# An attention loop in longer runs: two product runs and two runs of ten score tiles a slot

## The chip, the cores and the metric

The kernel runs on one core of one Trainium2 chip. The core has five engines that run side by side, each through its own queue in order: TensorE (PE in the profile, with its weight loads as PEld), VectorE (DVE), ScalarE (ACT), GpSimd (POOL) and SyncE (SP), which here only issues DMAs. The metric is the device time of the whole kernel in microseconds (us), the median of several runs.

## The reference

A transformer block on x of 8 batches, 1024 tokens and 512 features, all in fp32. First attention, then a mixture of eight experts:

```python
x = x + attention(layernorm(x))
x = x + experts(layernorm(x))

# attention: 16 heads of 32 features
theta_q = xh / (1 + abs(w_q)) + b_q + t * phi_q      # likewise theta_k; theta_v has no t
Q = concat(cos(theta_q), sin(theta_q))               # 64 features a head; K likewise
V = cos(theta_v) + sin(theta_v)
attn = softmax(causal(Q @ K.T / sqrt(64)))
theta_out = (attn @ V) / (1 + abs(w_out)) + b_out
return cos(theta_out) + sin(theta_out)

# experts: softmax router, the best two of eight, at most 160 tokens an expert and batch
h = relu(buf @ W1[e] + b1[e]); y = h @ W2[e] + b2[e]   # weighted and summed per token
```

Sine and cosine come from a table of 2048 entries with linear interpolation. The kernel computes them as an angle, a square and a hardware sine.

## The kernel before

**Work and stages.** The attention part is a loop of 32 **slots** (line 1736), n = 4b + c: batch b, and c one of four groups of 128 features, that is four heads. Two heads make a **pair**; a slot has pair 0 and pair 1. After the loop comes the expert part (`experts`), which the change leaves alone. For batch b - 1 a **router** runs inside the slots of batch b, as a generator that is advanced a step at a time (`route_on`, line 1764).

**Order.** VectorE, ScalarE, TensorE and SyncE have a manual schedule: each engine runs its instructions exactly in the order in which the Python code emits them. The code is therefore an order written out by hand. Generators are used to emit pieces of one piece of work between pieces of another: `some(k, g)` emits k steps, `rest(g)` all that are left. Waits between engines follow from the tiles that the instructions read and write.

**Scores.** `scores` (line 675) makes ten tiles for a pair: three for the first half of the queries, seven for the second. A tile is a set of matmuls (line 684) of 64 rows of the array, the two heads beside each other, on the diagonal also a mask product in bf16 (line 698), into a PSUM slot of two banks (`two_banks`, pool `ps_sc` of **three slots**, used in rotation), and one exp on ScalarE (line 704) into a tile `e` in SBUF. Transposes, the router's features and the router's sums use the same three slots.

**Products.** `attend` (line 710) multiplies the `e` tiles by v (line 718), 64 columns of the array a head, sums in PSUM, and one VectorE operation brings the result out (`av_sb`, line 726). One call makes half of the queries of a pair. `turn` (line 742) transposes a pair's two results on TensorE (line 216) and divides by the sums on VectorE (lines 753 and 755).

**Places.** `qk_pre` (line 508) transposes x for a later slot (line 216), and four VectorE operations (line 525) make angles in `qk_f`. `angle` (line 438) makes `qk_r`. `both` emits on ScalarE two squares (line 442) and two absolutes (line 585), `qk_sin` the sines (lines 594 and 445). `qk_post` (line 599) multiplies cosine half and sine half on VectorE (line 448), each followed by four DMAs that bring the result into the pair tiles `qk` for the scores. The position part of the angle comes by DMA (`load_base`, line 500).

**v and the output.** `v_pre` (line 619) has three VectorE operations for the angle and one shift; `sine`, `square` on ScalarE and `v_post` (line 639) finish v. `o_pre` (line 643) and `o_post` (line 651) do the same for the attention's output, with the residual and the statistics for the second layernorm (line 661).

**The router** (line 787): statistics and rows on VectorE (lines 798, 813), `features` transposes rows (line 216) and copies them out on VectorE (line 838), `sums` multiplies by the router's weights (line 875) and gathers (line 858) with copies on VectorE (lines 880, 882), then the choice of two experts and a product for each token's place (line 858 again, read at lines 966 and 967). It begins in the slot with c = 0 (`begin`), and the next slot finds `begin` set.

The profile shows two table loads a slot on ScalarE (1283 ns each), one ahead of the sines and one ahead of the exps that follow them.

Of the kernel before, what the change touches and what calls it, by code (L numbers as in the profile page):

```python
# [12 lines left out]
F32 = mybir.dt.float32  # L13
# [9 lines left out]
P = 128  # L23
# [51 lines left out]
def preln_attn_moe_kernel(  # L75
# [21 lines left out]
    nc = tc.nc  # L97
# [612 lines left out]
    def attend(n, pr, h, es, halves):  # L710

        vt = v_tiles[n % 2]
        av = ps_av.tile([P, 512], F32, name="av")
        tiles = tiles_of(h)
        for i, parts in enumerate(tiles):
            for kb, q0, w, at in parts:
                for a in range(2):
                    nc.tensor.matmul(  # L718
                        av[a * 64 : (a + 1) * 64, q0 - 512 * h :],
                        lhsT=vt[:, kb, 2 * pr + a, :], rhs=es[i][:, a, at : at + w],  # L720
                        start=kb == 0, stop=i + 1 == len(tiles),
                    )
# [1008 lines left out]
    last = None  # L1731
    o_st = route = first_rows = None
    begin = False
    place, angles, residual = [None], iter(()), iter(())
    first_gather = gather(0)
    for n in range(NCK):
        more, late = n + 1 < NCK, last is not None
        b, c = divmod(n, NCH)
        if n == NCK - 1:
            to_inputs.close()  # L1740
            first_rows = experts_begin()
        pos_n = trig.tile([P, S], F32, name="o_p")
        if n == NCK - 2:
            find_rows(0)
            next(first_gather)
        if late:
            e11, halves1, pos = last
# [33 lines left out]
        if n == 0:  # L1781
            some(2, *ahead)
        if n == 0 or begin:

            qk_st = rest(qk_pre(n + 1))
            if begin:
                v_post(n, v_st)
                next(route)
            angle(*qk_st)
            angles = keep(place, both(qk_st))  # L1790
            if begin:
                load_base(n + 2)

        if begin:
# [7 lines left out]
        if begin:  # L1802
            rest(asides.pop(0))
            v_st = v_box[0]
        elif more:
            v_st = v_box[0]
# [6 lines left out]
        if begin:  # L1813
# [11 lines left out]
        route_on(1)  # L1825
        if n == 2:
            load_b1()
        if c == 3 and b > 0:
            next(route)
            if b > 1:  # L1830
                fetch_slots(b - 2)
            if b < B - 1:
                scatter()


        some(3, *products)
        if n == 0:
# [23 lines left out]
        if late:  # L1861
            square(o_st[0])
            residual = o_post(n - 1, o_st)
        some(2, *ahead)
        begin = c == 0 and late
        if begin:
            rest(residual)
            route = router(b - 1)
            next(route)
        elif n + 2 < NCK:  # L1870
            route_on(1)
            qk_st = rest(qk_pre(n + 2))

        if c != 1:
            next(residual, None)
        if n + 2 < NCK and not begin and c != 1:
            angle(*qk_st)
        if c != 1:
            rest(residual)
        if c == 1:  # L1880
# [6 lines left out]
        route_on(1)  # L1887
        if c == 1:

            angle(*qk_st)  # L1890
        some(5, *ahead)
        if n + 2 < NCK and not begin:
            angles = keep(place, both(qk_st))
            some(2, angles)
            if n + 3 < NCK:
                load_base(n + 3)
        last = (es[1], halves1, pos_n)
# [62 lines left out]
```

## Time and profile before

| what | value |
|---|---|
| median of 3 runs | 3190.2 us (3189.37 to 3190.49) |
| the profiled execution | 3177.95 us, span 3176.2 us |
| granted TensorE clock | 0.998 |
| TensorE busy | 3112.0 us, 98% |
| VectorE busy | 2303.7 us, 73% |
| ScalarE busy | 1680.4 us, 53% |
| exps, line 704 | 569.4 us in 640 |
| score matmuls, line 684 | 598.3 us in 3072 |
| product matmuls, line 718 | 523.4 us in 3072 |

The profiled execution is one run and was 0.4% under the median of the others. Busy times are unions: where two matmuls run beside each other in two halves of the array they count once. A row of the profile names the line, the engine, the operation, what it writes and reads, the shape, how often it came (x), the busy time and the mean of one in ns, and the idle time before it with what ended it. A line of the timeline gives start, duration, engine, line, operation and count of merged instructions, and in brackets how long the engine was idle before and what released it. A busy TensorE can hold hidden waits, since the ends of matmuls are modelled; the starts are measured.

### The profile page before, as it was taken

How to read it: one execution, taken by the hardware profiler on the slowest of the kernel's cores; microseconds unless marked ns; L12 is line 12 of the kernel's file. 1: busy time of each engine (PE TensorE's matmuls, PEld its weight loads, DVE VectorE, ACT ScalarE, POOL GpSimd, SP SyncE). 2: the span in 40 equal slices, each digit the busy share in tenths (PEclk: the TensorE clock that was granted, in tenths of full speed). 3: DMA queues.
4: the chain of work that ended last, by engine and by line, in shares of the span. 5: the costliest groups of instructions: out<-in, count | busy, mean ns of one | idle time of the engine just before them, and what ended most of it. 6: DMA issues, size and time to landing. Idle time of an engine off the chain costs nothing.

```text
span 3176.2 us, 52225 instructions
## 1 busy us (share of the span) xinstructions
PE 3112.0 (98%) x20086; PEld 2147.5 (68%) x20086; DVE 2303.7 (73%) x4808; ACT 1680.4 (53%) x2599; POOL 424.1 (13%) x387
## 2 busy tenths in 40 slices
PE   5999999999999999999999999999999999999998
PEld 2444444444444444689699699699698698698697
DVE  8888878887887775738658658658667767767765
ACT  7888888888888885413423423423423423423423
POOL 3000202020201122410110110110110110110010
PEclk9999999999999999999999999999999999999999
DMA  5535454555545352533523523523533433433421
GB/s 167 147 100 166 106 165 132 148 138 149 164 133 160 80 167 55 149 82 96 155 54 91 152 57 95 145 59 98 140 64 100 132 67 102 128 67 108 118 58 23
DMA packets 288552, 358.79 MB, mean 113 GB/s; under 512 B 28376, under 2 KB 199088, under 8 KB 276272
## 3 DMA queue, kind: packets, MB, share of 16 engines
q1 hardware_dynamic: 264944, 312.20, 33.7%
q0 software_dynamic: 22912, 43.22, 7.3%
q8 instruction: 160, 2.62, 0.4%
q14 instruction: 88, 0.72, 0.1%
q10 hardware_dynamic: 448, 0.02, 0.0%
HBM read 207.02 MB, written 81.22 MB: 91 GB/s over the span
## 4 chain that ended last, share of the span: by engine, by line
PE 78%; DVE 4%; ACT 1%; issue 1%; DMA 0%; SPq 0%; POOLq 0%; POOL 0%; DVEq 0%; ACTq 0%
PE ps_p L1238 30%; PE ps_p L1474 10%; PE ps_p L1537 10%; PE av L718 10%; PE ps_s L684 9%; PE ps_p L1352 8%; ACT e L704 1%; PE ps_s L216 1%; PE ps_s L698 1%; DVE qk_f L525 1%; DVE qk_r L448 0%; DMA qk<-qk_r 0%; DVE xT L838 0%; DVE xe L1174 0%; DVE xe_s L1186 0%
## 5 line engine op out<-in xcount | busy, mean ns | idle before, releaser
L704 ACT ACTIVATE e<-ps_s 128x1024 f32<-128x1024 f32 (+1 forms) x640 | 569.4, 937 | 183.5 <-PE ps_s L684 110.0
L684 PE MATMUL ps_s<-qk 64*128 64x512 f32 (+3 forms) x3072 | 598.3, 506 | 28.2 <-DMA qk<-qk_r 12.4
L718 PE MATMUL av<-e,v 128*64 128x512 f32 (+3 forms) x3072 | 523.4, 490 | 0.0
L684 PEld LDWEIGHTS ps_s<-qk 64*128 64x128 f32 x3072 | 262.3, 188 | 216.0 <-issue 106.9
L718 PEld LDWEIGHTS av<-e,v 128*64 128x64 f32 x3072 | 200.5, 137 | 283.0 <-issue 267.0
L1238 PE MATMUL ps_p<-xe,w 128*128 128x256 f32 (+1 forms) x1024 | 317.6, 433 | 1.1 <-issue 1.1
L1238 PE MATMUL ps_p<-xe_s,t 128*128 128x256 f32 (+1 forms) x1024 | 317.6, 433 | 0.0
L1238 PE MATMUL ps_p<-xe,t 128*128 128x256 f32 (+1 forms) x1024 | 317.6, 433 | 0.0
L1316 POOL DMA_INDIRECT out_dram<-y,slots x80 | 127.8, 1597 | 1261.3 <-ACT y L1311 1017.8
L769 POOL DMA_INDIRECT slot_d<-token,slot x128 | 156.6, 1223 | 997.3 <-issue 620.8
L1238 PEld LDWEIGHTS ps_p<-xe_s,t 128*128 128x128 f32 x1024 | 194.4, 190 | 81.4 <-issue 0.8
L1238 PEld LDWEIGHTS ps_p<-xe,t 128*128 128x128 f32 x1024 | 194.2, 190 | 80.4 <-issue 0.4
L1238 PEld LDWEIGHTS ps_p<-xe,w 128*128 128x128 f32 x1024 | 193.7, 190 | 79.4 <-issue 1.2
L1281 DVE TENSOR_TENSOR hid<-hid 128x256 f32<-128x256 f32 (+1 forms) x128 | 63.9, 499 | 206.4 <-ACT hid L1279 206.4
L1537 PE MATMUL ps_p<-w_t,hid 128*128 128x256 f32 x960 | 212.4, 379 | 0.8 <-DVE y L1590 0.8
L1537 PEld LDWEIGHTS ps_p<-w_t,hid 128*128 128x128 f32 x960 | 180.0, 190 | 24.4 <-DVE y L1590 1.2
L1238 PE MATMUL ps_p<-xe_s,w 128*128 128x256 f32 (+1 forms) x512 | 158.9, 433 | 0.6 <-ACT p L1254 0.6
L1352 PE MATMUL ps_p<-w,hid 128*128 128x256 f32 x640 | 142.9, 379 | 0.0
L1474 PE MATMUL ps_p<-w,hid 128*128 128x128 f32 x1104 | 141.8, 275 | 0.0
L698 PEld LDWEIGHTS <-keys_b 64*128 64x128 bf16 x1536 | 80.9, 95 | 89.7 <-issue 71.8
L1311 ACT ACTIVATE y<-y,slots 128x256 f32<-128x256 f32 (+1 forms) x120 | 65.9, 578 | 142.8 <-DVE y L1389 105.5
L1474 PEld LDWEIGHTS ps_p<-w,hid 128*128 128x128 f32 x1104 | 135.8, 192 | 2.3
(289 smaller groups left out, 5182.7 us busy)
## 6 DMA issues: line engine op xcount, KB each, us to landing
w<-in_L_ffn_W_dram SPq DMA_DIRECT2D x256, 256.0 KB, 3.4
w<-in_L_ffn_W_dram SPq DMA_DIRECT2D x64, 512.0 KB, 6.8
qk<-qk_c SPq DMA_DIRECT2D x124, 256.0 KB, 4.5
qk<-qk_r SPq DMA_DIRECT2D x120, 256.0 KB, 4.9
qk_base<-base_d SPq DMA_DIRECT2D x28, 1024.0 KB, 8.8
xn_d<-xn SPq DMA_DIRECT2D x72, 256.0 KB, 2.3
rows_d<-xg SPq DMA_DIRECT2D x70, 256.0 KB, 2.1
x_mid<-in_L_attn_x_dram SPq DMA_DIRECT2D x16, 1024.0 KB, 9.2
```

The source lines that it names most:

```text
L684: nc.tensor.matmul(ps[:, a, at : at + w], lhsT=pair[r, 1, kb * P : (kb + 1) * P], rhs=pair[r, 0, q0 : q0 + w], start=at == 0, stop=not own ...
L698: nc.tensor.matmul(out_, lhsT=keys_b[r, part, :], rhs=late, start=False, stop=part == 1, skip_group_check=True,)
L704: nc.scalar.activation(e, ps[:, :, :n], AF.Exp, scale=UNIT * UNIT / math.sqrt(2 * DH))
L718: nc.tensor.matmul(av[a * 64 : (a + 1) * 64, q0 - 512 * h :], lhsT=vt[:, kb, 2 * pr + a, :], rhs=es[i][:, a, at : at + w], start=kb == 0, ...
L769: queued = nc.gpsimd.indirect_dma_start(out=slot_d[b], out_offset=bass.IndirectOffsetOnAxis(ap=idx, axis=0), in_=src, in_offset=None,)
L1238: nc.tensor.matmul(ps, lhsT=weights[:, k, :], rhs=rows[:, k, :], start=first and k == 0, stop=last and k == 1, skip_group_check=True,)
L1281: TT(g1, g3, h22, ALU.add)
L1311: nc.scalar.activation(part, part, AF.Identity, scale=meta[:, e, jj[r], 1:2].bitcast(F32))
L1316: ins = nc.gpsimd.indirect_dma_start(out=out, out_offset=bass.IndirectOffsetOnAxis(ap=meta[:, e, jj[r], 0:1], axis=0), in_=y, in_offset=No ...
L1352: nc.tensor.matmul(ps, lhsT=hid[:, k, part, cols], rhs=ws[weight][:, k, :], start=first and k == 0, stop=last and k == NHQ - 1, skip_group ...
L1474: nc.tensor.matmul(ps, lhsT=left[:, k, :], rhs=right[:, k, :], start=first and k == 0, stop=k == 3, skip_group_check=True,)
L1537: nc.tensor.matmul(ps[:, b * DC : (b + 1) * DC], lhsT=hid[:, k, part, b * P : (b + 1) * P], rhs=ws[weight][:, k, :], start=first and k == ...
```

## The change

The loop is put in another order. No instruction of the computation is added or taken away, except one: an exp of one element, emitted after the sines in every slot but the first.

- **Products.** Before, four runs a slot: the first three tiles of what was left of the slot before's pair 1, later its last four; all ten of pair 0 beside the sines; the first three of pair 1 inside its scores. After, two runs: all of the slot before's pair 1 at the start of a slot, all of pair 0 in the middle.
- **Scores.** Before, runs of five tiles with products between. After, ten tiles in a row for each pair, with the VectorE work of asides, residual and router steps emitted between them.
- **Transposes.** `qk_pre` for the next slot and `turn` of the slot before's pair 0 go ahead of the first product run. Before, `qk_pre` ran a slot sooner, in the second score run, and `turn` of pair 0 stood there too.
- **Squares and places.** `square` of v, `square` of o (now of slot n - 2's output), and `both` are emitted ahead of the first product run. In the slot where the router begins, and in the last, the square of o stays in the second score run.
- **v.** `v_pre` is emitted a slot sooner, behind `v_post` in the second score run; where `begin` is set, both come at the start of the slot, behind `angle`.
- **DMAs.** `load_base` goes to the start of the slot, `load_mid` stays in the second score run. The last half of `qk_post`, with its four DMAs, is emitted straight after the middle product run, ahead of the router's step there.

```diff
         products = [attend(n, 0, h, es[h], halves[0]) for h in range(2)]
-        if late:
-            products.insert(0, attend(n - 1, 1, 1, e11, halves1))
         ahead = [scores(pairs[0], h, es[h]) for h in range(2)]
-        v_box = [None]
-        asides = [keep(v_box, v_pre(n + 1))] if more else [first_rows]
+        asides = [] if more else [first_rows]
...
+        if n == 0:
+            some(2, *ahead)
+        if more:
+            qk_st = rest(qk_pre(n + 1))
         if late:
-            some(3, *products)
-        route_on(1)
+            es1, halves1, halves0 = last
+            pos = trig.tile([P, S], F32, name="o_p")
+            turn(0, halves0, pos)
+        if more:
+            angle(*qk_st)
+        if begin:
+            v_post(n, v_st)
+            v_st = rest(v_pre(n + 1))
+        if n and n + 2 < NCK:
+            load_base(n + 2)
+        if n == 2:
+            load_mid(b)
+        if late:
+            if more and not begin:
+                square(v_st[0])
+            if n > 1 and not begin:
+                square(o_st[0])
+                residual = o_post(n - 2, o_st)
+            if more:
+                rest(keep(place, both(qk_st)))
+            for h in range(2):
+                rest(attend(n - 1, 1, h, es1[h], halves1))
+        for _ in range(2):
+            route_on(1)
+        route_on(2)
+        with_asides(1)
         route_on(2)
         if c == 2 and route is not None:
             asides.append(part(route))
...
-        if begin:
-            some(5, *ahead)
-        else:
-            with_asides(5)
+        with_asides(4)
         rest(residual)
         for _ in range(2):
             route_on(1)
-        rest(angles)
...
+        if n == 0 or begin:
             square(v_st[0])
-        if late:
-            some(4, *products)
-        route_on(1)
-        route_on(1)
-        with_asides(5)
-        if begin:
-            square(v_st[0])
+        with_asides(2)
+        for _ in range(2):
+            route_on(1)
+        with_asides(3)
...
         if late:
             sine(o_st[1])
+        if n:
+            nc.scalar.activation(warm, split_c, AF.Exp)
...
         some(NTT, *products)
-
-        es, halves1 = [[], []], []
-        ahead = [scores(pairs[1], h, es[h]) for h in range(2)]
+        next_pairs = rest(post) if more else None
+
+        es1, halves1 = [[], []], []
+        ahead = [scores(pairs[1], h, es1[h]) for h in range(2)]
         route_on(1)
         route_on(2)
-        some(2, *ahead)
-        turn(0, halves[0], pos_n)
-        next_pairs = rest(post) if more else None
-        some(1, *ahead)
-        if late:
+        some(3, *ahead)
+        begin = c == 0 and late
+        if begin or not more:
             square(o_st[0])
-            residual = o_post(n - 1, o_st)
-        some(2, *ahead)
-        begin = c == 0 and late
+            rest(o_post(n - 1, o_st))
         if begin:
-            rest(residual)
             route = router(b - 1)
             next(route)
-        elif n + 2 < NCK:
-            route_on(1)
-            qk_st = rest(qk_pre(n + 2))
...
+        some(2, *ahead)
+        route_on(1)
+        if c == 1 and b > 0:
             load_mid(b)
...
         if more and not begin:
             v_post(n + 1, v_st)
-        some(3, attend(n, 1, 0, es[0], halves1))
...
+            if n + 2 < NCK:
+                v_st = rest(v_pre(n + 2))
         some(5, *ahead)
...
+        last = (es1, halves1, halves[0])
         pairs = next_pairs
-    rest(attend(NCK - 1, 1, 1, es[1], halves1))
+    pos_n = trig.tile([P, S], F32, name="o_p")
+    turn(0, halves[0], pos_n)
+    for h in range(2):
+        rest(attend(NCK - 1, 1, h, es1[h], halves1))
     turn(1, halves1, pos_n)
```

More of the change, by code (lines that the diff above doesn't have):

```diff
@@ L1733, in preln_attn_moe_kernel @@
     begin = False
-    place, angles, residual = [None], iter(()), iter(())
+    place, residual = [None], iter(())
     first_gather = gather(0)
@@ L1741, in preln_attn_moe_kernel @@
             first_rows = experts_begin()
-        pos_n = trig.tile([P, S], F32, name="o_p")
         if n == NCK - 2:
@@ L1745, in preln_attn_moe_kernel @@
             next(first_gather)
-        if late:
-            e11, halves1, pos = last
         es, halves = [[], []], [[], []]
         products = [attend(n, 0, h, es[h], halves[0]) for h in range(2)]
-        if late:
-            products.insert(0, attend(n - 1, 1, 1, e11, halves1))
         ahead = [scores(pairs[0], h, es[h]) for h in range(2)]
-        v_box = [None]
-        asides = [keep(v_box, v_pre(n + 1))] if more else [first_rows]
+        asides = [] if more else [first_rows]
         if b == 0 and c in (1, 2):
@@ L1780, in preln_attn_moe_kernel @@
             asides.append(part(route))
-        if n == 0:
-            some(2, *ahead)
-        if n == 0 or begin:
-            qk_st = rest(qk_pre(n + 1))
-            if begin:
[L1787 to L1790, printed above, removed]
-            if begin:
-                load_base(n + 2)
-        if begin:
-            some(5, *ahead)
-        else:
-            with_asides(5)
+        with_asides(4)
         rest(residual)
@@ L1800, in preln_attn_moe_kernel @@
             route_on(1)
-        rest(angles)
[L1802 to L1806, printed above, removed]
-            square(v_st[0])
-        if late:
-            some(4, *products)
-        route_on(1)
-        route_on(1)
-        with_asides(5)
-        if begin:
-            square(v_st[0])
+        if n == 0:
+            rest(keep(place, both(qk_st)))
+            v_st = rest(v_pre(1))
+        if n == 0 or begin:
+            square(v_st[0])
+        with_asides(2)
+        for _ in range(2):
+            route_on(1)
+        with_asides(3)
         for g in asides:
@@ L1823, in preln_attn_moe_kernel @@
             o_st = o_pre(n - 1, pos)
-        route_on(1)
-        route_on(1)
+        for _ in range(2):
+            route_on(1)
         if n == 2:
@@ L1851, in preln_attn_moe_kernel @@
         some(NTT, *products)
-        es, halves1 = [[], []], []
-        ahead = [scores(pairs[1], h, es[h]) for h in range(2)]
+        next_pairs = rest(post) if more else None
+        es1, halves1 = [[], []], []
+        ahead = [scores(pairs[1], h, es1[h]) for h in range(2)]
         route_on(1)
         route_on(2)
-        some(2, *ahead)
-        turn(0, halves[0], pos_n)
-        next_pairs = rest(post) if more else None
-        some(1, *ahead)
-        if late:
+        some(3, *ahead)
+        begin = c == 0 and late
+        if begin or not more:
             square(o_st[0])
-            residual = o_post(n - 1, o_st)
-        some(2, *ahead)
-        begin = c == 0 and late
+            rest(o_post(n - 1, o_st))
         if begin:
-            rest(residual)
             route = router(b - 1)
             next(route)
-        elif n + 2 < NCK:
-            route_on(1)
-            qk_st = rest(qk_pre(n + 2))
[L1874 to L1880, printed above, removed]
+        some(2, *ahead)
+        route_on(1)
+        if c == 1 and b > 0:
             load_mid(b)
@@ L1885, in preln_attn_moe_kernel @@
             v_post(n + 1, v_st)
-        some(3, attend(n, 1, 0, es[0], halves1))
-        route_on(1)
-        if c == 1:
-            angle(*qk_st)
+            if n + 2 < NCK:
+                v_st = rest(v_pre(n + 2))
         some(5, *ahead)
[L1892 to L1897, printed above, removed]
+        last = (es1, halves1, halves[0])
         pairs = next_pairs
-    rest(attend(NCK - 1, 1, 1, es[1], halves1))
+    pos_n = trig.tile([P, S], F32, name="o_p")
+    turn(0, halves[0], pos_n)
+    for h in range(2):
+        rest(attend(NCK - 1, 1, h, es1[h], halves1))
     turn(1, halves1, pos_n)
```

## The prediction

> **What bounds the kernel now.** I read the page from the top: busy shares, the slices, the costliest groups, then the order of time inside single slots. The change touches the attention loop alone, the first 1,170 us or so (15 of 40 slices).
>
> ```profile
> PE 3112.0 (98%) x20086; PEld 2147.5 (68%) x20086; DVE 2303.7 (73%) x4808; ACT 1680.4 (53%) x2599; POOL 424.1 (13%) x387
> ...
> PE   5999999999999999999999999999999999999998
> ...
> DVE  8888878887887775738658658658667767767765
> ACT  7888888888888885413423423423423423423423
> ```
>
> TensorE sets the end, but in these slices ScalarE and VectorE run at 0.8 beside it, so an order that is bad for them is paid on TensorE. A busy PE also hides waits (ends are modelled), so I go by starts of matmuls.
>
> ```profile
> 611.21 0.20 PEld L718 LDWEIGHTS av<-e,v 128*64 128x64 f32 x4 [0.76 <-issue]
> 611.69 0.14 PEld L718 LDWEIGHTS av<-e,v 128*64 128x64 f32 x2 [0.29 <-issue]
> 612.12 0.14 PEld L718 LDWEIGHTS av<-e,v 128*64 128x64 f32 x2 [0.29 <-issue]
> ...
> 614.37 0.30 PEld L684 LDWEIGHTS ps_s<-qk 64*128 64x128 f32 x4 [0.39 <-ACT qk_c L585]
> 614.91 0.19 PEld L684 LDWEIGHTS ps_s<-qk 64*128 64x128 f32 x2 [0.24 <-issue]
> 615.34 0.19 PEld L684 LDWEIGHTS ps_s<-qk 64*128 64x128 f32 x2 [0.23 <-issue]
> ```
>
> 512-column passes follow each other every 0.43 us, but the first of a product run takes 0.48 and the first of a score run 0.54; the first start after a turn of the array (128*64 to 64*128 or back) is 0.10 late besides (by single starts: the last 256 product columns begin at 650.03 and stream 0.21, the score begins at 650.34). So **score to product costs 0.15, product to score 0.21, a pair 0.36 us**. A clean slot (c=3, 35.88 us from one set of transposes to the next) has four pairs: 1.44. Its real waits are only 0.3 (0.10 and 0.22, before matmuls whose PSUM slot an exp still held).
>
> **ScalarE beside it.** Exps that follow each other start 0.92 us apart (1024 elements; 1.02 long) or 0.49 (512). A pair's ten tiles take ScalarE 8×0.92+2×0.49=8.34. On TensorE a 512-column tile is 0.86; with the mask products the ten (T1 to T10) are 0.93, 1.01, 0.51, 4×0.86, 0.93, 1.01, 0.51 = 8.34. **A run of ten is balanced to the hundredth**, with three PSUM slots between. From the timeline an exp starts 0.27 after its tile, and a slot is filled again 0.22 after its exp's end.
>
> **The change: array turns.** Four product runs and four score runs a slot become two and two: two pairs, −0.72 a slot. In a batch with a router the trace of before has 34 turns (32+2). After, the sums of groups 0 and 1 and the last gather lie inside score runs (S0, S1, S4, two turns each): 16+6=22. Six pairs saved: **−2.2 us a router batch** (seven of them), −0.72 in each of four slots before the first router.
>
> **A run of ten, walked.** From its start: T1 done 1.04 (with 0.11), exps at 1.31, 2.32, 3.24, 3.73, 4.65, 5.57, 6.49, 7.41, 8.34, 9.26. T5 needs the slot of exp 2: 2.32+1.02+0.22=3.56, a wait of 0.14; T10 ends at 8.58. Now transposes follow: the first set wants exp 8's slot (8.65: 0.07), a second set exp 9's (9.58 against 9.25: 0.33). The slot's first run has one set behind it, the second has two (qk_pre, turn): 2×(0.14+0.07)+0.33=**0.75 a slot, where a clean slot had 0.3**. Clean slots: −0.72+0.45=−0.27.
>
> [...] By the rows it costs the 0.45 only, because 8.34 meets 8.34; but nothing in ten tiles catches up, so what delays an exp delays TensorE one for one.
>
> **Is ScalarE free when a run starts?** Behind run 1 lie turn(1) and products(n,0) (0.6+7.7, ending at 17.1); ScalarE does the sines and the new one-element exp. Its row is line 201, 0.20 us; bounds 0 and 0.26 (the 64-element exp).
>
> ```profile
> 651.58 4.39 ACT L704 ACTIVATE e<-ps_s 128x1024 f32<-128x1024 f32 x5 [0.27 <-PE ps_s L684]
> 655.99 1.28 ACT L594 ACT_TABLE_LOAD   x1
> 657.28 2.00 ACT L594 ACTIVATE qk_c<-qk_c,quarter_c 128x2048 f32<-128x2048 f32 x1
> ...
> 663.00 1.28 ACT L704 ACT_TABLE_LOAD   x1
> ```
>
> From 655.99 to 664.28 is 8.3; last exp done 9.85, so ready at 18.4; the next T1 can be read at 18.5. Hidden, by 0.1 us. [...]
>
> Behind run 2 come squares of v (1.04) and o (1.04), then the place's two squares and two absolutes (2.08+1.9). These wait for the angle: transposes 8.65–9.25, four placements to 12.2, turn's two operations to 13.2, angle 14.4; absolutes end 18.5, first exp possible 19.4 (products end 18.0). Hidden, margin 0.9; each us beyond is a us on TensorE.
>
> v_pre (four DVE operations, 3.1 us) a slot sooner falls in run 2 after v_post and ends by about 7.2, before the placements at 9.5: free in clean slots. qk_pre a slot later has only the margin above. load_base (1 MB, 8.8 us to land) is issued after those placements and wanted 35 us later; SP has nothing behind it until the next pair DMAs. Pair DMAs (8, landing 4.5 and 4.9) are issued straight after the products, used 15 us later. load_mid and load_x stay in run 2, behind pair DMAs; POOL's scatters keep their places and nobody on the path waits for them. All zero; a late pair would cost its lateness. The first slot and the tail issue the same instructions in another order, TensorE's sum unchanged: zero, a few us either way.
>
> **VectorE where the router begins** is where cover is gone. c=0, second run, from its start:
>
> ```profile
> 973.51 1.22 DVE L448 SCALAR_TENSOR_TENSOR t_r<-o_p,t_r 128x1024 f32<-128x1024 f32 x1
> 974.76 1.22 DVE L658 SCALAR_TENSOR_TENSOR x_mid<-t_r,x_mid 128x1024 f32<-128x1024 f32 x1
> ...
> 981.01 1.00 DVE L813 TENSOR_SCALAR xn<-x_mid,mv,rstd 128x512 f32<-128x512 f32 x2
> ...
> 983.11 1.29 DVE L838 COPY xT<-ps_s 128x512 f32<-128x512 f32 x2 [0.45 <-PE ps_s L216]
> 984.32 2.72 DVE L525 SCALAR_TENSOR_TENSOR qk_f<-ps_s,inv_qk,qk_base 128x512 int32<-128x512 f32 x4
> ```
>
> Residual to rows took 8.5 us. After the change it starts at 5 (the square of o sits behind exp 3) and ends at 13.5. In order on VectorE then: placements 16.2, turn 17.1, angle 18.3, v_post 19.4, v_pre 22.5, two av_sb 23.9, and only then the copies of the first router features, 25.2. Before, those copies came ahead of the placements. Slots rotate by three: features, T1, T2, and **T3 waits for these copies**. TensorE gets to T3 at 21.8 (run 2 9.5, transposes, products 11.4–19.1, features, T1, T2) and starts at 25.3: **3.5 us**. TensorE's queue is in order, so the other tiles and the products stand behind T3, and ScalarE's exps behind them. The wait also covers ScalarE's absolutes, which end at 22.4.
>
> The same rotation is visible where it now costs less:
>
> ```profile
> 1020.56 0.41 DVE L880 COPY lg<-ps_s 128x256 f32<-128x256 f32 x1
> 1020.89 0.16 DVE L882 TENSOR_TENSOR prob<-ps_s,br_b 128x16 f32<-128x16 f32 x1
> ...
> 1021.20 1.13 PE L684 MATMUL ps_s<-qk 64*128 64x512 f32 x4 [0.57 <-DVE prob L882]
> ```
>
> After, the last half of the place product (`rest(post)`, 2.2 us) stands ahead of such reads: with products ending at 0, av_sb to 0.9, this to 3.1, sums read at 3.6: T3 at 3.75 instead of 2.85, **0.9** (c=1). For the router's places (c=2) 3.95 instead of 2.5, **1.45**.
>
> Further: the square of o inside c=0's run, **1.04**; features and sums inside c=1's first run, **0.65** (T6 and the third features each about 0.3 behind an exp; v's square lies in the hole that the sums leave); gather and small exp at c=2, 0.2.
>
> **Sum**, router batch: 4×0.75+3.5+0.9+1.45+1.04+0.65+0.2, less 0.2 where a T3 wait replaces T5's: 10.5 us of waits. Before: by starts in the batch from 862.0 to 1014.2 (152.2 us, of which 140.7 is streaming), 5.1. Difference 5.4, less 2.2: +3.2. Seven batches +22.4, four slots without router −1.1: **+21 us**. The profiled execution took 3177.95 us (span 3176.2, 1.75 around it), giving 3199; the runs' median stands 12.25 above, so **3190.2+21=3211**.
>
> **Rivals.**
> - **The turns decide: faster.** If VectorE's backlog at c=0/c=1 is shorter, or the copies are reached earlier, the three T3 waits (5.85 a batch) go: 3.2−5.85=−2.65, ×7, −1.1: −20, **3171**. It decides from 3.2 us less wait a batch on. For: turns are certain. Against: VectorE's order is written out, and the trace shows T3-type waits already.
> - **Waits and turns cancel: 3184 to 3197.** The T3 wait is half of mine, or the waits of before were of the kind that go.
> - **ScalarE becomes the bound: slower still.** 0.1 us of margin in one run and 0.9 in the other is thin. 0.4 late in each of 64 runs is +26: **3237**. For: in a run of ten no lateness is made good. Against: exps and loads fit on paper.
> - **It does not make two runs:** the router's sums cut them; counted, 22 turns instead of 16.
>
> **How the numbers follow.** Main case 0.57 (own range 3199 to 3226), turns decide 0.17, cancel 0.10, ScalarE 0.16. A measurement here tells 0.2%, 6.4 us. Faster 0.17; slower 0.57+0.16, less a little at the edge, 0.72; same 0.11. The range 3177 to 3242 leaves out the far ends of the second and fourth case, about 0.1 each side.
>
> **What would show it.** Right: 22 turns a router batch; clean slots near 35.6; score matmuls of c=1 waiting on DVE xT (line 838) for some 3 us, and on prob and spot for about 1; waits for exp at the transposes (line 216). Wrong: clean slots above 36.2, with exps that start late behind sines or absolutes (ScalarE's case), or c=1 without the xT wait (turns decide).

## The result, and the profile after

The changed kernel takes **3227.4 us** (median of 4 runs, 3221.7 to 3227.8) against 3190.3 us: 37 us more, a ratio of 1.0112 (95% interval 1.0095 to 1.0130). Slower, as forecast; the forecast was 3211.

The head of the page and the waits of TensorE (engine, line, what it waited for: us in total, times, longest), first of the kernel after, then of the kernel before:

```profile
PE 3114.4 (97%) x20086; PEld 2155.2 (67%) x20086; DVE 2309.3 (72%) x4808; ACT 1680.1 (52%) x2630; POOL 420.0 (13%) x387
...
PE   5999999999999999999999999999999999999998
...
DVE  8887878787877776646767767767767668657665
ACT  7878888878787876413323323323423423423423
```

```profile
PE ps_s L684 <- ACT e L704: 23.6, 24, 3.7
PE ps_s L684 <- DVE tmp L966: 14.5, 7, 2.1
...
PE ps_s L684 <- DVE xT L838: 8.0, 7, 1.2
PE ps_s L216 <- ACT e L704: 6.1, 36, 0.3
PE ps_s L684 <- DVE prob L882: 5.1, 8, 0.7
```

```profile
PE ps_s L684 <- ACT e L704: 4.8, 3, 3.7
PE ps_s L684 <- DVE prob L882: 4.8, 10, 0.6
...
PE ps_s L216 <- ACT e L704: 1.4, 8, 0.3
```

Busy times hardly move: apart from the 31 one-element exps no engine does more. What is new is that score matmuls (L684) wait seven times, once a router batch, for VectorE to read the tokens' places (L966) and the features (L838), and some twenty times more for an exp. From here on, "by starts" means: the start of a matmul, less the start of the one before it and the time that this one's columns take to stream (512 fp32 columns 0.43 us, the distance of one pass from the next at full clock). The first matmul of the expert part starts at 1301.2 instead of 1259.7: the loss is in the loop. A second execution of the same kernel, taken beside the experiments, has 1294.8, and the part behind the loop is there as long as before (1906.8 and 1906.7). The first one's loop is 6.4 us longer still, of which 6.8 us more at half clock (below) are 3.4, and it has in addition one stall of 6.5 us of TensorE near 1380, behind the loop. So the accounts below are made on the second, while the lines shown are of the first, where these waits are the same: **+35.1 us in the loop**, of a difference of medians of 35.9.

**Where the router's places are read (c=2).** The timeline of the kernel after, TensorE, VectorE and ScalarE:

```profile
438.62 2.00 ACT L594 ACTIVATE qk_c<-qk_c,quarter_c 128x2048 f32<-128x2048 f32 x1
...
441.37 0.25 DVE L753 RECIPROCAL rec<-ps_s 128x16 f32<-128x16 f32 x1
...
444.36 1.06 ACT L445 ACTIVATE t_r<-t_r 128x1024 f32<-128x1024 int32 x1 [0.99 <-DVE t_r L438]
...
445.43 1.28 ACT L1844 ACT_TABLE_LOAD   x1
446.72 0.20 ACT L1844 ACTIVATE warm<-split_c 128x1 f32<-128x1 f32 x1
446.83 2.54 ACT L704 ACTIVATE e<-ps_s 128x1024 f32<-128x1024 f32 x3
...
447.77 2.28 DVE L448 SCALAR_TENSOR_TENSOR qk_r<-qk_f,qk_r 128x2048 f32<-128x2048 f32 x1
447.89 0.70 PE L684 MATMUL ps_s<-qk 64*128 64x256 f32 x4 [0.74 <-ACT e L704]
449.96 0.21 DVE L966 TENSOR_TENSOR tmp<-hot,ps_s 128x64 f32<-128x64 f32 x1
...
450.47 0.22 DVE L966 TENSOR_TENSOR tmp<-hot,ps_s 128x64 f32<-128x64 f32 x1
...
450.74 6.26 PE L684 MATMUL ps_s<-qk 64*128 64x512 f32 x20 [2.07 <-DVE tmp L966]
```

Two things are late. The sine of the output waited 0.99 for VectorE, which had done the router's choice first (the reciprocal of `turn` comes only at 441.37), so the first exp is late and the third tile starts 0.91 late by starts. And the two reads of the places (L966, the second ends at 450.69) stand behind the last half of the place product (L448, 2.28), so the fourth tile starts another 2.23 late.

**Where the features are copied (c=1),** same view:

```profile
540.79 1.99 ACT L585 ACTIVATE qk_c<-qk_r 128x1024 f32<-128x1024 int32 x2
542.69 2.54 ACT L704 ACTIVATE e<-ps_s 128x1024 f32<-128x1024 f32 x3
543.03 1.40 DVE L726 TENSOR_SCALAR av_sb<-av,inv_o 128x512 f32<-128x512 f32 x2
543.74 0.70 PE L684 MATMUL ps_s<-qk 64*128 64x256 f32 x4 [1.50 <-ACT e L704]
544.35 1.28 DVE L838 COPY xT<-ps_s 128x512 f32<-128x512 f32 x2
545.67 3.05 PE L684 MATMUL ps_s<-qk 64*128 64x512 f32 x8 [1.15 <-DVE xT L838]
```

The exp is late behind the absolutes (L585), and the copies (L838) behind `av_sb` and what precedes it: 1.67 and 1.31 by starts, 2.98 together.

**The clock.** The granted clock is the share of its full speed that TensorE was given, 1.00 or, in some stretches, 0.50. Busy time by stretch around c=2 (stretch and its length; PE, PEld, DVE, ACT, POOL busy with counts; granted TensorE clock; DMA share; GB/s):

```profile
444.08:447.49 3.41, 3.07 (x42) 1.53 (x38) 3.41 (x4) 3.11 (x4) 0.00 (x0) 1.00 0.00 0
447.49:450.90 3.41, 0.95 (x10) 0.66 (x12) 3.31 (x7) 1.86 (x3) 0.00 (x0) 1.00 0.80 154
450.90:454.31 3.41, 3.41 (x10) 1.37 (x12) 3.34 (x5) 1.02 (x1) 0.00 (x0) 0.50 1.00 257
454.31:457.73 3.42, 3.42 (x24) 1.65 (x22) 1.04 (x2) 3.21 (x4) 0.00 (x0) 1.00 0.91 216
```

Straight behind the wait the granted clock is 0.50 for 3.41 us: a busy TensorE gets through 10 matmuls there. TensorE counts as wholly busy there; only the clock and the starts (passes 0.85 apart instead of 0.43) tell. Apart from one in the first slot (at 60.89 in the trace of before, at 61.77 here, 6.83 us in both), which is left out of all counts, the loop of the kernel before has no such stretch. The kernel after has nine in its first execution (one of them twice as long) and eight in the second. By estimate from these, a stretch of 3.41 us is worth 3.41/2 = 1.7 us; by starts, they make 14.0 us of the second execution's 35.1.

The clean slot (c=3), by contrast, is better than before: its transposes come 35.26 us apart, where the kernel before needs 35.9.

```profile
458.53 0.67 PE L216 MATMUL ps_s<-ident,xn 64*128 64x64 f32 x16
...
493.79 0.71 PE L216 MATMUL ps_s<-ident,xn 64*128 64x64 f32 x16
```

### The profile page after: what moved, and what is told of

Read it like the earlier page. It is cut to its first block, busy times and chain, and to the rows that moved or that the text cites. A ratio compares the mean times of both kernels' runs of the same rounds, so it can differ in the third digit from the quotient of the medians.

```text
span 3226.0 us, 52455 instructions
## 1 busy us (share of the span) xinstructions
PE 3114.4 (97%) x20086; PEld 2155.2 (67%) x20086; DVE 2309.3 (72%) x4808; ACT 1680.1 (52%) x2630; POOL 420.0 (13%) x387
## 4 chain that ended last, share of the span: by engine, by line
PE 73%; DVE 11%; ACT 11%; issue 3%; DMA 1%; another core or an unknown queue 0%; SPq 0%; POOLq 0%; ACTq 0%; POOL 0%; DVEq 0%
PE ps_p L1238 30%; PE ps_p L1474 10%; PE ps_p L1537 10%; PE av L718 8%; PE ps_p L1352 8%; PE ps_s L684 7%; ACT e L704 6%; PE ps_s L216 1%; DVE st_mid L661 1%; ACT qk_c L594 1%; DVE av_sb L726 1%; ACT t_r L445 1%; ACT qk_r L445 1%; DVE qk_f L525 1%; DVE x_mid L658 1%
## 5 line engine op out<-in xcount | busy, mean ns | idle before, releaser
L684 PE MATMUL ps_s<-qk 64*128 64x512 f32 (+3 forms) x3072 | 598.2, 513 | 64.7 <-ACT e L704 23.6
L704 ACT ACTIVATE e<-ps_s 128x1024 f32<-128x1024 f32 (+1 forms) x640 | 559.1, 943 | 114.4 <-PE ps_s L698 53.9
L718 PE MATMUL av<-e,v 128*64 128x512 f32 (+3 forms) x3072 | 509.5, 488 | 0.0
L684 PEld LDWEIGHTS ps_s<-qk 64*128 64x128 f32 x3072 | 267.2, 191 | 256.6 <-ACT e L704 102.5
L726 DVE TENSOR_SCALAR av_sb<-av,inv_o 128x512 f32<-128x512 f32 x128 | 94.8, 745 | 84.8 <-PE av L718 80.7
```

Source lines behind the costliest of these rows:

```text
L684: nc.tensor.matmul(ps[:, a, at : at + w], lhsT=pair[r, 1, kb * P : (kb + 1) * P], rhs=pair[r, 0, q0 : q0 + w], start=at == 0, stop=not own ...
L704: nc.scalar.activation(e, ps[:, :, :n], AF.Exp, scale=UNIT * UNIT / math.sqrt(2 * DH))
L718: nc.tensor.matmul(av[a * 64 : (a + 1) * 64, q0 - 512 * h :], lhsT=vt[:, kb, 2 * pr + a, :], rhs=es[i][:, a, at : at + w], start=kb == 0, ...
```

## The experiments

Three theories. **W, the waits:** TensorE stands before tiles whose PSUM slot a late VectorE operation still has to read; VectorE's order at c=1 and c=2 makes it late; the half clock follows those waits. **S, the long runs themselves:** ten tiles in a row leave ScalarE no slack, so the loss stays when VectorE's order is mended. **C, the clock:** the half clock belongs to the new order of matmuls, whatever the waits. Every kernel is compared with the kernel before, run on the same chip in the same comparison. Its own time was 3176.9 to 3177.2 us beside the first eight kernels and 3190.9 beside the last four; so ratios are what to compare. Between these two groups even a ratio is good to some 0.15% only: in the traces of the last four the part behind the loop is 8 to 10 us longer than in those of the first eight, the kernel before was 13.8 us slower there and was not profiled, and why is open. The column "expert part begins" (in us, from one trace each) is free of this; it moves by some 1 us with the first slot.

| kernel | time, us | ratio to before (95%) | expert part begins | half-clock stretches in the loop |
|---|---|---|---|---|
| after, again | 3213.1 | 1.0115 (1.0098 to 1.0132) | 1294.8 | 8 |
| router's read first | 3190.3 | 1.0039 (1.0026 to 1.0052) | 1270.4 | 3 |
| v behind the features | 3199.4 | 1.0064 (1.0048 to 1.0081) | 1280.1 | 5 |
| both moves | 3174.2 | 0.9990 (0.9981 to 0.9999) | 1256.5 | 0 |
| both, choice behind the output | 3174.3 | 0.9989 (0.9980 to 0.9998) | 1256.5 | 0 |
| both, rows behind the angle | 3201.8 | 1.0071 (1.0054 to 1.0088) | 1285.6 | 6 |
| the same, choice behind the output | 3198.9 | 1.0071 (1.0054 to 1.0088) | 1276.5 | 4 |
| before, place product first | 3188.6 | 1.0038 (1.0023 to 1.0052) | 1270.5 | 0 |
| before, longer wait | 3212.5 | 1.0065 (1.0048 to 1.0082) | 1285.7 | 2 |
| both, without the small exp | 3209.9 | 1.0058 (1.0041 to 1.0074) | 1281.5 | 0 |
| both, places later | 3179.3 | **0.9957** (0.9940 to 0.9973) | 1253.2 | 0 |
| the same, placements sooner | 3208.6 | 1.0055 (1.0038 to 1.0072) | 1280.6 | 5 |

Most stretches are 3.41 us long. Twice as long are two of the three with the router's read first, four of the six with the rows behind the angle, and three of the five in the last row.

**The router's read ahead of the last half of the place product.**

```diff
         some(NTT, *products)
+        route_on(1)
+        route_on(2)
         next_pairs = rest(post) if more else None
 
         es1, halves1 = [[], []], []
         ahead = [scores(pairs[1], h, es1[h]) for h in range(2)]
-        route_on(1)
-        route_on(2)
```

> The changed kernel with one move: after the middle product run the router's step is emitted ahead of the last half of the place product, so VectorE reads the sums (c=1) and the token places (c=2) 2.2 us sooner and gives their PSUM slot back sooner. Theory W (score tiles wait for PSUM slots that late VectorE reads hold, and each such wait is followed by a stretch at half clock): the waits of 0.8 us (c=1) and 2.2 us (c=2) go, 3.0 a router batch, 21 us in seven, and about four of the eight half-clock stretches inside the loop, 1.7 us each: 3227 goes to about 3200. Rival S (the runs of ten themselves are the cost, because ScalarE can't keep up over ten tiles): the tile waits for an exp instead, and the time stays within 5 us of 3227. Rival C (the half-clock stretches belong to the order and not to the waits): 3206, with as many stretches as before.

Against the changed kernel in a neighbouring comparison the time falls by 3213.1 - 3190.3 = 22.8 us. At c=2 one wait of 1.67 is left of 3.1, the sums' wait at c=1 is gone, and no half-clock stretch follows c=2 any more; the three left are all at c=1, where the wait is untouched (1.66 + 1.31 in the second batch). At c=1 the changed kernel has four stretches in its first execution and one in its second, with the same waits; what decides that is left open. For W, and against C.

**v's work behind the copies of the features.**

```diff
-        if begin:
-            v_post(n, v_st)
-            v_st = rest(v_pre(n + 1))
         if n and n + 2 < NCK:
             load_base(n + 2)
...
         for _ in range(2):
             route_on(1)
+        if begin:
+            v_post(n, v_st)
+            v_st = rest(v_pre(n + 1))
         route_on(2)
         with_asides(1)
...
-        if n == 0 or begin:
+        if n == 0:
             square(v_st[0])
         with_asides(2)
+        if begin:
+            square(v_st[0])
```

> The changed kernel with one move: in the slot after the router's beginning, the end of v and the beginning of the next v (v_post, v_pre, 4.3 us of VectorE) are emitted behind the router's first feature copies instead of ahead of the placements' squares; the square of that next v goes two tiles later. Theory W: the tile that waited 1.3 us for the copy out of the features goes on at once, but the tile ahead of it waited 1.7 us for a first exp that came late behind the absolutes, and that wait stays, since the angle isn't earlier: 9 us in seven batches, and up to four half-clock stretches, 7 us: 3211 to 3218. The prediction's own reading (the copies are the wait, 3.5 us, and cover ScalarE): 3203 or less. Rival S: no change, 3227.

It gains 13.6 us. The wait for `xT` is gone (no line for L838 is left among the waits); at c=1 1.15 for the exp and 0.81 for a copy of sums (L880) are left of 1.67 and 1.31. The five stretches left are all at c=2, whose 0.91 and 2.23 are unchanged. The two experiments are mirror images: **each wait removed takes its half clock along.**

**Both moves together.**

> The changed kernel with both of the first two moves (the router's read ahead of the place product's last half; v_post and v_pre behind the first feature copies). By single starts the first move left batches of 153.4 us, the second 154.9, the changed kernel 158, the kernel before 152.2. Theory W: the waits are apart (c=2 and the end of c=1; the beginning of c=1), so the gains add but for the half-clock stretches: about 152 us a batch, within 0.3% of the kernel before, either side. Rival A (a gain of one move is the other's, since both only free VectorE at the same place): no better than the first move alone, 0.4% over the kernel before.

From 3213.1 to 3174.2: 38.9 us, a little more than the 22.8 + 13.6 of the single moves, and the loop has no half-clock stretch at all. The waits of TensorE:

```profile
PE ps_s L684 <- ACT e L704: 14.9, 18, 3.7
...
PE ps_s L684 <- DVE tmp L966: 10.5, 7, 1.5
PE ps_s L216 <- ACT e L704: 6.5, 38, 0.3
PE ps_s L684 <- DVE lg L880: 2.7, 7, 0.7
```

The runs of ten and the two product runs are as in the changed kernel, and so is ScalarE's order but for one square of v, two tiles later at c=1; what differs is VectorE's order at two places. That level with the kernel before (0.1% under it) is reached this way is against S as well as C.

**The choice behind the output's angle as well,** to take the 0.99 off the sine at c=2.

```diff
         with_asides(4)
-        rest(residual)
+        late_choice = c == 2 and route is not None
+        if late_choice:
+            next(residual)
+        else:
+            rest(residual)
...
             o_st = o_pre(n - 1, pos)
+        if late_choice:
+            for g in asides:
+                rest(g)
+            rest(residual)
```

> Both moves and the end of the choice and the residual's statistics behind the output's angle at c=2. Theory W: the last sine at c=2 comes 1 us sooner, so 0 to 1 us a batch, 0 to 7 us under the kernel with the two moves. Rival S: no change.

Nothing (3174.3). With the router's read moved, the third tile waits for that read, and the exp's lateness lies under it: the later of two sets the time, 1.66 with both moves, 1.53 here.

**The router's first step behind the next slot's angle,** so that the residual and the rows don't stand ahead of it; and the same with the choice moved.

```diff
             angle(*qk_st)
+        if begin:
+            next(route)
...
             route = router(b - 1)
-            next(route)
```

> Both moves before, and the router's first step (statistics, root and rows, 4.4 us of VectorE) from the second score run of c=0 to behind the angle of the next slot, so that the placements, the angle, the squares and the absolutes come 4.4 us sooner. Theory W: the late first exp at c=1 (1.7 us) goes too: against the changed kernel 3.0+3.0 us a batch, 42 us, and most of the half-clock stretches, 13 us; less what the later rows cost: 3172 to 3185, at or under the kernel before. Rival S: no better than 3215, since every run of ten still waits for exps. Rival C: 3185 to 3195, with half-clock stretches left.

> The kernel of the three moves, and at c=2 the statistics of the residual and the end of the router's choice (some 4 us of VectorE) behind the turn and the angle of the output instead of ahead of them, so that the last sine comes in time. Theory W: the sine of the output waits 1.0 us for VectorE at c=2 and the first exp of the next run is 0.7 to 0.9 late; that goes: 5 to 6 us less than without this move, 3167 to 3180. Rival S: no change to the kernel without this move.

Both miss: 27.7 and 24.8 us slower than both moves alone. The timeline at c=1 (rows behind the angle):

```profile
543.31 0.64 PE L875 MATMUL ps_s<-xT,wr_sb 128*32 128x256 f32 x8
...
544.18 1.29 DVE L626 TENSOR_TENSOR v_p<-xn,inv_v 128x512 f32<-128x512 f32 x2
545.51 1.22 DVE L631 TENSOR_TENSOR v_p<-v_p,bias_v 128x1024 int32<-128x1024 f32 x1
...
547.61 0.40 DVE L880 COPY lg<-ps_s 128x256 f32<-128x256 f32 x1
...
548.07 1.22 PE L684 MATMUL ps_s<-qk 64*128 64x512 f32 x2 [3.47 <-DVE lg L880]
```

The rows are later, so the features are; the sums that follow them are ready at 543.9, but v's work, which had been given that place, is in front of their copy (L880). A new wait of up to 4.3 us, 20.5 in all, and six stretches at half clock. The mend moved the wait one read further.

**The wait put into the kernel before.** Its short runs are kept, only the last half of the place product goes ahead of the router's step, as the change has it.

```diff
         some(NTT, *products)
+        next_pairs = rest(post) if more else None
 
         es, halves1 = [[], []], []
...
         turn(0, halves[0], pos_n)
-        next_pairs = rest(post) if more else None
```

> The kernel before, with the last half of the place product emitted straight behind the middle product run, ahead of the router's step, as the change has it; nothing else is changed, so the product runs stay four and the score runs stay short. Theory W: the sums at c=1 and the token places at c=2 hold their PSUM slots for 2.2 us more and score tiles wait, 0.8 and 1.5 to 2.2 us a batch, 16 to 21 us in seven, and 0 to 12 us of half clock behind them: 0.5 to 1.0% over the kernel before. Rival S (only long runs are hurt): under 0.2%, since short runs with products between make good what was late.

0.38% slower, under the 0.5 to 1.0% expected and over the 0.2% of S; 10.8 us in the loop (1270.5). Its waits at these places are 0.8 a batch at c=1 and 1.36 at c=2, and no stretch is at half clock. Without any long run the position of these two operations costs a third of the whole loss.

**A longer wait there:** five more VectorE operations of 0.46 us each (multiplications by one) ahead of the read at c=2.

```diff
         route_on(1)
+        if c == 2 and route is not None:
+            for _ in range(5):
+                nc.vector.tensor_scalar(bias_o, bias_o, 1.0, None, ALU.mult)
```

> The kernel before with the last half of the place product ahead of the router's step (that alone was 11.5 us over the kernel before, with waits of 0.8 and 1.36 us a batch and no half clock inside the loop), and at c=2 five operations of VectorE, 0.46 us each, that multiply a constant row by one, ahead of the read of the token places: the wait there grows from 1.4 to about 3.7 us. It tells whether the half clock follows a long wait or belongs to the changed order. If it follows the wait: the trace shows stretches at half clock of 3.4 us or more in the loop, up to seven, and the time is 16+(5 to 12) us over that kernel, 1.0 to 1.3% over the kernel before. If it belongs to the changed order: no stretch, and 16 us, 0.9%.

Both expected sizes were too high (0.65% over the kernel before, for 1.0 to 1.3 or 0.9). In the loop it is 15.2 us more than the run above (1285.7 against 1270.5): 3.4 are the two stretches, and 11.8 are left of the 16 that five operations in seven slots are. By the two ratios, which come from the two groups, it is 9. The wait did not grow to one long gap: transposes and a tile came in between (0.55 and 1.54). But two stretches at half clock appear, **in the order of before**, both at c=2, one of them right behind the wait shown here (TensorE's timeline, then the stretch from 294.00):

```profile
291.04 0.70 PE L684 MATMUL ps_s<-qk 64*128 64x256 f32 x4 [0.38 <-ACT e L704]
...
293.20 1.33 PE L684 MATMUL ps_s<-qk 64*128 64x512 f32 x4 [1.38 <-DVE tmp L966]
```

```profile
294.00:297.50 3.50, 3.50 (x24) 1.89 (x24) 0.39 (x2) 1.97 (x2) 0.00 (x0) 0.51 0.90 196
```

That ends C: the long order without the waits has no half clock, and the short order with them has it.

**Both moves, without the one-element exp,** which the prediction had costed at nothing.

```diff
-        if n:
-            nc.scalar.activation(warm, split_c, AF.Exp)
```

> The changed kernel with the first two moves, without the exp of one element behind the sines. It frees ScalarE of 0.2 us a slot. The prediction's sum: hidden, 0 us to 2 us in all. If the first exp of every second run is as tight as the prediction's margin of 0.1 us made it, up to 0.2 in each of 31 slots: 6 us faster.

Missed: 0.999 becomes 1.0058, some 22 us, and the loop is 25.0 us longer. The timeline with the small exp (both moves), then the same place without it:

```profile
658.50 1.28 ACT L1846 ACT_TABLE_LOAD   x1
...
659.80 0.20 ACT L1846 ACTIVATE warm<-split_c 128x1 f32<-128x1 f32 x1
...
660.03 2.60 ACT L704 ACTIVATE e<-ps_s 128x1024 f32<-128x1024 f32 x3
```

```profile
670.72 1.13 PE L684 MATMUL ps_s<-qk 64*128 64x512 f32 x4
...
672.01 1.28 ACT L704 ACT_TABLE_LOAD   x1 [1.52 <-PE ps_s L698]
...
673.31 2.43 ACT L704 ACTIVATE e<-ps_s 128x1024 f32<-128x1024 f32 x3
...
674.38 2.90 PE L684 MATMUL ps_s<-qk 64*128 64x512 f32 x12 [0.85 <-ACT e L704]
```

Without it, the table load belongs to the first exp and waits with it for the first score tile: ScalarE idles 1.52 and then loads for 1.28, while three tiles fill the slots and TensorE stops. With it the load is done by the time the tile is there. By the traces, 30 of these loads start 0.7 to 3.1 us late without it (1.5 in the median), and with it none more than 0.01. 25.0 us in the 31 slots that have it are 0.8 a slot: about 1.1 at c=0, c=1 and c=3, and nothing at c=2, where the third tile waits for the places anyway. The kernel before has no small exp, and its loads start within 0.02 of the sines' end all the same.

**Both moves, and the place product for the tokens behind the fifth tile of its run.**

```diff
         route_on(1)
-        route_on(2)
         next_pairs = rest(post) if more else None
...
         some(2, *ahead)
         route_on(1)
+        route_on(2)
         if c == 1 and b > 0:
```

> The changed kernel with the first two moves, and at c=2 the product for the token places is emitted behind the fifth score tile of the second run instead of ahead of the first. Theory W: the wait of 1.65 us at c=2 goes, for two more turns of the array (0.36): 1.3 a batch, 9 us, to 0.4% under the kernel before. If the turns cost more than the rows say, or the places' slot stalls later tiles as much: no gain, 0.1% under the kernel before as without this move.

**Faster than both kernels: 0.9957 of before.** At c=2 only 0.75 of a late exp is left, and the slot falls from 38.5 to 37.8 us; the wait for `tmp` is gone from the list. Of the 11.6 us to the kernel before, the traces show 6.5 in the loop (1253.2 against 1259.7), 0.2%; the rest is the difference between the groups that was named above, and is not explained. So it is partly luck that the ratio meets the 0.4% expected: against both moves the loop gains 3.3 us, where 9 were expected.

**The next slot's transposes and angle at c=0 ahead of the router's statistics.**

```diff
-        if more:
+        if more and not begin:
             qk_st = rest(qk_pre(n + 1))
...
+            qk_st = rest(qk_pre(n + 2))
+            angle(*qk_st)
             route = router(b - 1)
             next(route)
```

> The same, and where the router begins the transposes, placements and angle for the next slot stand in the second score run of c=0 ahead of the router's statistics, instead of at the next slot's start. Theory W: the late first exp at c=1 (1.41 us by single starts) goes, as the absolutes end 4 us sooner: 1 to 1.4 a batch, 7 to 10 us under the kernel without this, 0.6% under the kernel before. Against: the angle has to wait on VectorE for the DMA out of the sines' tile, some 10 us into the run, and holds the rows and the features: 0 or a loss of up to 1 us a batch.

Missed, 1.0055. The transposes now hold PSUM slots until VectorE has done the output's residual; in c=0's run:

```profile
520.19 2.71 DVE L525 SCALAR_TENSOR_TENSOR qk_f<-ps_s,inv_qk,qk_base 128x512 int32<-128x512 f32 x4
...
522.95 1.14 PE L684 MATMUL ps_s<-qk 64*128 64x384 f32 x8 [2.38 <-DVE qk_f L525]
```

Seven such waits, 16.6 us with an eighth, and the router's reads are later too (L880: 8.2 us). **The kernel after, once more,** is what the gains of the single moves and of both together are read against:

> The changed kernel itself, beside the others on one chip, since the kernel before took 3190 us on the first chip and 3177 on the second. All theories: 1.0 to 1.3% over the kernel before, as measured first; it is the base for the differences of this set.

## Why the prediction was right in sign and short in size

**The sum.** Forecast +21 us, measured +37 by medians and +35.1 in the loop of the second execution: 3227.4 is just above the main case's own range (3199 to 3226) and inside the whole one. Of these, 14.0 are stretches at half clock. Without them the loop would be 21.1 longer: the forecast's waits and turns were right in total, and the step that failed is one that the sum did not have. It took TensorE's streaming as it stood, at the granted clock of 0.998, and let every wait cost its own length. Here the waits cost their length, and eight times in the second execution a stretch at half clock followed, by estimate 1.7 us more each.

**By batch.** From 256.1 to 1202.7 are six router batches, 157.8 each, against 152.25: +5.5, of which the seven stretches in them make 2.0 (7×1.7/6). +3.5 is left, forecast +3.2. The total hides errors that cancel:

- **Turns.** 34 to 22 a batch, as counted. Right.
- **Clean slots.** Forecast -0.27, measured -0.6 (35.9 to 35.3). The waits of 0.14 before T5 and 0.07 before the first transposes do not show; the 0.33 before a second set of transposes does, in every slot (L216 for an exp: 1.4 us before, 6.1 after). 0.75 a slot should have been 0.35, 1.6 a batch too much.
- **Features at c=1.** 2.98 for 3.5. VectorE's queue was walked rightly, but the third tile waited for the exp of the first and only the fourth for the copies; the slots were not taken in strict rotation as I assumed. Which slot a tile gets is left open.
- **Sums at c=1.** 0.80 for 0.9. Right.
- **Places at c=2.** 3.1 for 1.45, the largest error among the waits. I had the read behind the place product, but took ScalarE to be free there; its sine waits for VectorE, which does the choice and the statistics before `turn`. Two late things add up where a third and a fourth tile each wait for one.
- **Square of o at c=0.** 0.62 for 1.04.

These corrections make the forecast 2.2 a batch instead of 3.2, and 3.5 was measured; 1.3 lies in smaller delays that I did not take apart. So the agreement of the total is partly luck.

**The small exp.** "Hidden, zero" was right for the kernel as it is and wrong as a reason. I asked what it costs; the question was what its absence costs. The margin of 0.1 us took the load to stand right behind the sines, and it stands there only because of this exp.

**The rivals.** "ScalarE becomes the bound", 3237, is nearer in number (10 us off, my main case 16) and not in mechanism: both moves together keep every run of ten, every sine and absolute where the change put them, and are level with before. "The turns decide" was given as 3171, ratio 0.994, once the waits go. With them mended the kernels stand at 0.999 and, with the places later, 0.9957: by the 0.18 that the prediction gave a turn, the turns save 18 us with both moves (170 in the loop for 268) and 15 with the places later (184), of which 3.2 and 6.5 are left in the loop. The rest still goes into waits, above all for exps (with both moves 21.4 us at L684 and L216, for 6.2 before). "Waits and turns cancel" is what both moves give.

**The signs named ahead.** The waits on `xT`, `prob` and at the transposes are on the page, with other sizes: `xT` 1.15 a batch for some 3, the places (as `tmp`, L966) 2.1 for about 1. Clean slots are not over 36.2. What the list of signs lacked was the granted clock.

## What to carry to other kernels

When an order written by hand is changed on a full TensorE, list every PSUM tile that another engine must empty, and walk that engine's queue up to each read: two places where VectorE's reads came to stand behind 2 to 5 us of its other work were the whole loss here, and moves that mend one read by delaying the next (rows behind the angle, placements sooner) lose as much again. Then read the granted clock behind the waits, not the busy share alone: here 0.91 and 2.23 us close together were followed by 3.41 us at clock 0.50 in five of seven batches of one execution and in all seven of another, and the single waits of up to 1.66 us that both moves leave were not. And where an activation needs another table, see whether an activation that is ready early can carry the load: here that was worth 25 us in 31 slots.

## What the runs showed of the hardware

**Half clock behind waits.** The nine stretches of the first execution of the kernel after last 3.41 us, the one at 229.02 twice that, at a granted clock of 0.50. Each stands behind waits: in the 3.41 us ahead of it TensorE was busy for 0.94 us (the one at 450.89) to 1.58 us (the one at 546.46). No single idle time was that long: between 100 and 1290 us the longest is 2.07, and ahead of 546.46 there were two, 1.50 and 1.15, with a short tile between. By starts, 0.91 and 2.23 at c=2 were followed by half clock in all seven batches of the second execution and in five of seven of the first, 1.67 and 1.31 at c=1 in one and in four of seven. One of the two at c=2 that were not: from 607.91 TensorE was busy for 1.53 of 3.41 us, with an idle time of 2.07, and the clock stayed at 1.00 behind it. So these figures give no limit, and what decides between two like waits is left open. The single waits of up to 1.66 us with both moves were not followed by half clock, nor were those of the kernel before, where the longest idle time between 100 and 1255 us is 0.9.

**A table load waited with the activation that it belonged to.** Without the one-element exp the load at 672.01 started 1.52 us late, where its activation waited for a matmul, and with it no load started more than 0.01 late; the loop was 25.0 us longer without it, over 31 slots.
